# Four edits at the program's end and in GpSimd's row chains of a four-layer graph kernel

## The chip, the cores and the metric

The kernel runs on one core of one Trainium2 chip. The metric is device time in microseconds (us) of one execution; of several runs the median is taken. Engines are named as in the profile: PE (TensorE), PEld (its weight loads), DVE (VectorE), ACT (ScalarE), POOL (GpSimd), SP (SyncE, which issues most DMAs).

## The reference, cut to what matters

Inputs are `x` [4096, 64] and a 0/1 adjacency matrix `adj` [4096, 4096], both float32. Four layers follow each other, each of the form `x = layernorm(x + L(x, adj))`:

```python
# layer 0: mean over neighbours
h = (adj @ x + x) / deg;  out = relu(concat([x, h]) @ W + b);  out = out / max(|out|, 1e-12)
# layers 1 and 3: attention in hyperbolic space (c = 1/r**2 in layer 1, c = 1 in layer 3)
x_t   = logmap0(x)
att   = sigmoid((x_t @ wl)[:, None] + (x_t @ wr)[None, :] + b) * adj          # [N, N]
local = logmap(x[:, None, :], x[None, :, :])                                  # every pair i, j
out   = proj(expmap(x, einsum('ij,ijd->id', att, local)))
# layer 2: neighbours weighted by 0.5 ** (their rank counted from the row's end), at most 100
out = w @ (x @ weight) + bias
```

`logmap` and `expmap` are made of dot products, norms, an artanh and a tanh. Per row of `x`, layers 1 and 3 so need sums over the 4096 neighbours (the heavy part), and after it a chain of operations on one number a row: three inverse square roots (of the tangent vector's squared norm, of the result's squared norm for `proj`, and of the variance for the layernorm), a tanh and a reciprocal.

## The kernel before

**Tiling.** The 4096 rows are 32 blocks of 128. The output rows are cut into four groups `s` of 1024 columns of the transposed adjacency matrix; a layer goes through them in the order 3, 2, 1, 0 (`GROUPS`). Within a group it goes through 16 pairs `g` of two blocks, `k = 1` and then `k = 0`. One load on SP's queue (`load`, six buffers) brings one pair's tile of `adj`, 128 x 2 x 1024 float32, 1 MB.

**A pair in layers 1 and 3** (`attend`, from L1064). For each of the two blocks PE fills a PSUM tile `z` of 128 x 1024 by six matmuls of 512 columns (L1098, L1101, L1104; there are three such tiles of two banks each). ACT makes `sig` (L1113) and the square `sq` of z (L1116); DVE makes t = max(z, 0) * sig (L1119). Once a pair, DVE completes both blocks together, t = (sq + const) * t, over 2048 columns (L1121). PE then multiplies t with the neighbours' rows and adds into the PSUM tile `acc` (`add_up`, L1076, four matmuls a pair, two pairs behind the current one; what is left over follows after the last pair). ACT copies the group's sums to SBUF (L1127, `sums`).

**The rows of a group** (`move`, L1137 to L1270). PE turns the sums into rows and centres them (L1168, in two parts through the one bank `aux`), ACT copies each part out (L1179), and then come w = x*u (L1184), u squared (L1185, ACT), their sums over 64 columns (L1187, L1189, DVE) and some 80 operations on 128 x 8 numbers: one for each row of the group. They end in two large products (L1265, L1266) and their sum (L1269), which is the next layer's `x` of that group. For the last group, 0, these operations run on DVE; for groups 3, 2 and 1 the small ones and the large products run on GpSimd (class `Small`, whose `stt` is two GpSimd operations at L749 and L750), save the reductions, the reciprocal (L1233) and the seed of each root (L762), which stay on DVE. In a root, L766 to L774 are the Newton steps; `rsqrt` (from L720) is the same root for the other rows on DVE, such as those of `prepare` and `norm_rows`, which make a layer's operands ready.

```python
def pool_done(small, large=0):           # units to wait for GpSimd
    if place[0] == 2:                    # place[0] is the layer
        return 2 + int((small * 0.29 + large) / 1.45)
    return 2 + int(small * 0.33 + large)
...
def soon():
    return 0 if place[0] in (0, 2) else 1
```

**Order of the work.** PE's and ACT's instructions run in the order in which the program issues them; the order on DVE and GpSimd is a scheduler's, held behind the pairs. The pair loop calls `tick` after each block and each pair. Each call advances the row work, which is written as Python generators in two queues (`later`, `in_turn`): the number that a generator yields is the number of ticks until its next piece is issued. In layers 1 and 3 `near()` and `soon()` are one tick; `pool_done(small, large)`, and `Small.wait` through it, estimate from numbers of small and large GpSimd operations how many ticks to leave before DVE or ACT needs their result. `free` waits until the bank `aux` is not held. So a group's chain is issued among the pairs of the next group; that of group 0 of layer 3 has nothing beside it.

**Around it.** Layer 2 makes its supports (`supports`, L1298 to L1319) as groups of layer 1 become ready, and its own rows (`end_2`, L1556 among others, a 256-column product with a PSUM operand). After layer 3 each group's rows are stored (`store`, L1692 to L1695: groups 1 and 0 on SP's queue, 3 and 2 on ACT's). The program's end also has a check, `fits` (L1706 to L1719), transposed by PE (L1733) and loaded into a register that decides a branch.

Of the kernel before, what the change touches and what calls it, by code (L numbers as in the profile page):

```python
# [49 lines left out]

LN2 = 0.6931471805599453
ROOT2 = 2.0**0.5
LOG = (0.3333341, 0.1998662, 0.14984541)
OFF_EDGE = 255.0
CUT = 27.0
# [5 lines left out]
def gnn_stack_kernel(  # L61
# [509 lines left out]
    def stream(fits):  # L571

        with ExitStack() as st:
# [74 lines left out]
            def soon():  # L648


                return 0 if place[0] in (0, 2) else 1
# [7 lines left out]
            def near():  # L659

                return 3 if place[0] == 0 else 1
# [58 lines left out]
            def rsqrt(a, name):  # L720

                n = a.shape[1]
                r, t = nums(name, n), nums("rs_t", n)
                V.tensor_scalar(
                    r.bitcast(I32), a.bitcast(I32), -0.5, float(0x5F3759DF), ALU.mult, ALU.add
                )
                for _ in range(3):
                    V.tensor_mul(t, r, r)
                    V.scalar_tensor_tensor(t, t, -0.5, a, ALU.mult, ALU.mult)
                    V.scalar_tensor_tensor(r, t, 1.5, r, ALU.add, ALU.mult)  # L730
                return r

            class Small:
# [18 lines left out]

                def wait(self, small, large=0):

                    return pool_done(small, large) if self.on_pool else soon()

                def rsqrt(self, a, name, small):

                    r, t = self.nums(name), self.nums("rs_t")
                    if self.on_pool:  # L760
                        yield self.wait(small)
                    V.tensor_scalar(  # L762
                        r.bitcast(I32), a.bitcast(I32), -0.5, float(0x5F3759DF),
                        ALU.mult, ALU.add,
                    )
                    for _ in range(3):  # L766
                        self.mul(t, r, r)
                        if self.on_pool:
                            self.mul(t, t, a)
                            self.ts(t, t, -0.5, 1.5, ALU.mult, ALU.add)  # L770
                            self.mul(r, t, r)
                        else:
                            self.stt(t, t, -0.5, a, ALU.mult, ALU.mult)
                            self.stt(r, t, 1.5, r, ALU.add, ALU.mult)  # L774
                    return r


# [286 lines left out]
            def attend(layer, s, rate, then):  # L1064

                left_b = left_bs[s]

                acc = ps.tile([P, W], F32, name="acc")
                lag = []

                def add_up(g, t, behind=None):

                    for k in (1, 0):
                        j = 2 * g + k
                        for h in range(2):
                            it = nc.tensor.matmul(  # L1076
                                acc[h * D : (h + 1) * D, :], xe[:, j, :],
                                t[:, k, h * W : (h + 1) * W],
                                start=j == BLOCKS[0], stop=j == BLOCKS[-1],
                            )  # L1080
                            if behind is not None:
                                in_order(it.ins, behind.ins)

                for g in reversed(range(NB // 2)):
                    _, edge = load(s, g)
                    need((layer, 2 * g // WB))
                    if g == 4 and then is not None:
                        later(in_turn((layer, then, "left"), spread_left(then)), True)
                    for k in (1, 0):
                        j = 2 * g + k  # L1090
                        of = slice(j * P, (j + 1) * P)

# [14 lines left out]
                        if k == 1:  # L1107
                            if len(lag) == 2:
                                add_up(*lag.pop(0), last)
                            sq = sb.tile([P, 2, WW], F32, name="sq")  # L1110
                            t = sb.tile([P, 2, WW], F32, name="t", bufs=3)
                        sig = sb.tile([P, WW], F32, name="sig", bufs=3)
                        nc.scalar.activation(  # L1113
                            sig, left_b, AF.Sigmoid, bias=right[:, j : j + 1]
                        )
                        nc.scalar.activation(  # L1116
                            sq[:, k], zp, AF.Square, bias=ROOT + OFF, scale=-1.0 / UNIT
                        )
                        V.scalar_tensor_tensor(t[:, k], zp, 0.0, sig, ALU.max, ALU.mult)  # L1119
                        tick(rate)  # L1120
                    V.scalar_tensor_tensor(t, sq, HIGH**2, t, ALU.add, ALU.mult)  # L1121
# [5 lines left out]
                nc.scalar.copy(sums, acc)  # L1127
                return sums
# [8 lines left out]
            def move(layer, s, sums, curve):  # L1137
# [55 lines left out]
                G.mul(k, k, rb[:, at])  # L1193

# [68 lines left out]
                G.mul(q, q, r)  # L1263
                yield soon()
                E.tensor_mul(w, xg, over(p))  # L1265
# [519 lines left out]
```

## Time and profile before

| what | us |
|---|---|
| median of 3 runs (lowest to highest) | 1074.26 (1074.15 to 1074.6) |
| the profiled execution, its own time | 1069.06 |
| its span | 1067.3 |
| busy in the span: PE / PEld / DVE / ACT / POOL | 982.1 / 403.2 / 920.2 / 754.3 / 270.8 |
| mean granted PE clock | 0.971 |
| DMA traffic | 271.62 MB, 254 GB/s |

In the span, layer 0 takes about 0 to 198 us, layer 1 to 517, layer 2 to 717 and layer 3's pairs to 1038; the last row chain and the store follow. The span is the part of the execution that the profiler's records cover; 1.76 us of the execution's own time lie around it. The profiled execution is a single one, 5.2 us shorter than the median of the runs; lengths of instructions are read from it, and differences are formed against its own time.

A line of the timeline gives start, duration, engine, line, operation, output<-inputs with their shapes, and in brackets the engine's idle time before it with the releaser, the instruction that ended the wait. A line of the table by stretch gives the stretch and its length, the busy time and count of instructions of PE, PEld, DVE, ACT and POOL, the mean granted PE clock (1.00 is full speed), the mean share of the 16 DMA engines and GB/s. Line numbers are those of the kernel before, unless the text says otherwise.

### The profile page before, as it was taken

To read this page: it belongs to the slowest core of one execution; us is meant where nothing else is said; L and a number is where in the kernel's file an instruction comes from. 1 tells how busy PE (TensorE), PEld (TensorE's weight loads), DVE (VectorE), ACT (ScalarE), POOL (GpSimd) and SP (SyncE) were. 2 spreads that over 40 slices of the span, in tenths; PEclk is the share of its full clock that TensorE was granted. 3 is DMA by queue.
4 is the path that set the end of the run, shared out by engine and by line. 5 is a ranking of instruction groups with operands and counts; after the bars stand their busy time and mean duration, and the time that the engine had idled before them with its cause. 6 is when DMAs were issued, how large, how long until landed. Compare 5 with 4: busy or idle time off the path is not lost.

```text
span 1067.3 us, 13569 instructions
## 1 busy us (share of the span) xinstructions
PE 982.1 (92%) x4760; PEld 403.2 (38%) x4845; DVE 920.2 (86%) x1501; ACT 754.3 (71%) x877; POOL 270.8 (25%) x649
## 2 busy tenths in 40 slices
PE   5997998789999999999999999998899999999980
PEld 2454554333333333333333344443333333333320
DVE  8577887899999999999485489849999999999976
ACT  0013122779988899888677788898898888898850
POOL 0011212010044515435500010101102454444163
PEclk8899999989999999999999999999999999999985
DMA  9999999745656656757598999996465766666300
GB/s 364 356 426 364 383 395 375 277 175 197 233 204 230 215 206 202 249 184 249 205 363 332 371 346 316 324 321 222 138 236 190 250 216 208 241 228 234 131 1 24
DMA packets 38580, 271.62 MB, mean 254 GB/s; under 512 B 4710, under 2 KB 4710, under 8 KB 5734
## 3 DMA queue, kind: packets, MB, share of 16 engines
q1 hardware_dynamic: 37728, 270.03, 69.3%
q8 instruction: 40, 0.66, 0.2%
q10 hardware_dynamic: 774, 0.63, 0.2%
q14 instruction: 38, 0.31, 0.1%
HBM read 269.58 MB, written 1.05 MB: 254 GB/s over the span
## 4 chain that ended last, share of the span: by engine, by line
PE 66%; DVE 22%; ACT 5%; DMA 2%; POOL 2%; issue 2%; ACTq 0%; SPq 0%; POOLq 0%
PE acc L1076 17%; PE z L1641 11%; PE z L1101 8%; PE z L1098 7%; PE z L1104 7%; DVE t L1119 7%; DVE t L1121 6%; PE acc L1465 6%; PE z L1653 3%; DVE junk L844 2%; PE z L1607 2%; DMA edges<-in_adj_dram 2%; ACT sq L1648 1%; ACT sq L1116 1%; POOL sq L1435 1%
## 5 line engine op out<-in xcount | busy, mean ns | idle before, releaser
L1119 DVE SCALAR_TENSOR_TENSOR t<-z,sig 128x1024 f32<-128x1024 f32 x256 | 309.7, 1218 | 16.9 <-ACT sq L1116 14.9
L1121 DVE SCALAR_TENSOR_TENSOR t<-sq,t 128x2048 f32<-128x2048 f32 x128 | 295.2, 2306 | 0.2
L1116 ACT ACTIVATE sq<-z 128x1024 f32<-128x1024 f32 x256 | 254.3, 1021 | 56.5 <-PE z L1104 21.6
L1113 ACT ACTIVATE sig<-left_b,right 128x1024 f32<-128x1024 f32 x256 | 286.9, 1149 | 5.3 <-DVE t L1119 4.5
L1076 PE MATMUL acc<-t,xe 128*64 128x512 f32 x1024 | 260.4, 614 | 10.9 <-DVE t L1121 9.3
L1101 PE MATMUL z<-lo_hi,hi_lo 128*128 128x512 f16 x512 | 193.7, 378 | 3.8 <-issue 0.9
L1104 PE MATMUL z<-dst,src 74*128 74x512 f16 x512 | 194.7, 380 | 0.0
L1098 PE MATMUL z<-edges,two_i 128*128 128x512 bf16 x463 | 181.7, 392 | 5.4 <-DVE t L1119 5.4
L1648 ACT ACTIVATE sq<-z 128x512 bf16<-128x512 f32 (+1 forms) x192 | 137.6, 740 | 40.1 <-PE z L1641 39.5
L1076 PEld LDWEIGHTS acc<-t,xe 128*64 128x64 f32 x1024 | 64.3, 137 | 140.6 <-issue 106.5
L1098 PEld LDWEIGHTS <-two_i 128*128 128x128 bf16 x512 | 50.2, 98 | 120.7 <-issue 74.5
L1465 PE MATMUL acc<-edges,first 128*128 128x512 bf16 x241 | 77.9, 400 | 16.5 <-DMA edges<-in_adj_dram 15.9
L1641 PE MATMUL z<-edges,pass_by 128*128 128x512 bf16 x240 | 84.7, 388 | 7.3 <-ACT sq L1648 6.0
L844 DVE SCALAR_TENSOR_TENSOR t<-edges 128x2048 bf16<-128x2048 f32 x32 | 73.0, 2287 | 19.6 <-DMA edges<-in_adj_dram 19.2
L1641 PE MATMUL z<-edges,enter 128*128 128x512 bf16 x251 | 86.8, 387 | 0.5
L844 DVE SCALAR_TENSOR_TENSOR junk<-edges 128x2048 bf16<-128x2048 f32 x32 | 73.1, 2284 | 13.1 <-DMA edges<-in_adj_dram 13.1
L1465 PE MATMUL acc<-edges,third 128*65 128x512 bf16 x256 | 80.9, 397 | 0.8 <-issue 0.2
L1104 PEld LDWEIGHTS <-src 74*128 74x128 f16 x512 | 49.1, 96 | 72.0 <-issue 9.2
L1101 PEld LDWEIGHTS <-hi_lo 128*128 128x128 f16 x512 | 50.2, 98 | 60.6 <-issue 14.5
L901 POOL TENSOR_TENSOR sq<-z 128x512 f32<-128x512 f32 x8 | 10.2, 1278 | 156.1 <-DVE z L900 144.8
L1184 POOL TENSOR_TENSOR w_att<-x,u 128x512 f32<-128x512 f32 x6 | 12.7, 2121 | 140.9 <-ACT u L1179 140.9
L1607 PE MATMUL z<-sq,halves 128*128 128x512 bf16 x120 | 45.1, 377 | 0.7 <-ACT sq L1648 0.5
(399 smaller groups left out, 965.0 us busy)
## 6 DMA issues: line engine op xcount, KB each, us to landing
edges<-in_adj_dram SPq DMA_DIRECT2D x256, 1024.0 KB, 4.9
x<-in_x_dram SPq DMA_DIRECT2D x4, 256.0 KB
out_dram<-x ACTq DMA_DIRECT2D x2, 256.0 KB
out_dram<-x SPq DMA_DIRECT2D x2, 256.0 KB
w_sb<-in_L_gnn_W_dram ACTq DMA_DIRECT2D x1, 32.0 KB, 4.8
w_twice<-in_L_gnn_weight_dram ACTq DMA_DIRECT2D x2, 16.0 KB, 4.8
given<-in_L_gnn_b_dram ACTq DMA_DIRECT2D x1, 0.2 KB
given<-in_L_gnn_bias_dram ACTq DMA_DIRECT2D x1, 0.2 KB
```

The lines of the kernel that those rows point to most:

```text
L844: V.scalar_tensor_tensor(junk, a, 0.0, a, ALU.not_equal, ALU.not_equal, accum_out=odd[:, n : n + 1])
L1076: it = nc.tensor.matmul(acc[h * D : (h + 1) * D, :], xe[:, j, :], t[:, k, h * W : (h + 1) * W], start=j == BLOCKS[0], stop=j == BLOCKS[-1],)
L1098: nc.tensor.matmul(half, two_i, edge[:, at : at + W], start=True, stop=False)
L1101: nc.tensor.matmul(half, hi_lo[:, of], lo_hi[:, to], start=False, stop=False)
L1104: last = nc.tensor.matmul(half, src[:, of], dst[:, to], start=False, stop=True)
L1113: nc.scalar.activation(sig, left_b, AF.Sigmoid, bias=right[:, j : j + 1])
L1116: nc.scalar.activation(sq[:, k], zp, AF.Square, bias=ROOT + OFF, scale=-1.0 / UNIT)
L1119: V.scalar_tensor_tensor(t[:, k], zp, 0.0, sig, ALU.max, ALU.mult)
L1121: V.scalar_tensor_tensor(t, sq, HIGH**2, t, ALU.add, ALU.mult)
L1465: nc.tensor.matmul(accs[h][:m], lhs[:, j, :], edge[:, at : at + W], start=j == BLOCKS[0], stop=j == BLOCKS[-1],)
L1641: nc.tensor.matmul(z[:, h : h + W], lhs, rhs[:, h : h + W], start=j == BLOCKS[0], stop=True, skip_group_check=True,)
L1648: weighed[0] = nc.scalar.activation(w, z[:, :n], AF.Exp, bias=-(OFF_EDGE + CUT) * LN2, scale=-LN2)
```

## The change

Four edits, in the diff's order of lines:

- *Roots.* Each inverse square root starts from the same integer seed, and takes one step of third order and one Newton step where it took three Newton steps: seven DVE operations after the seed for nine, ten GpSimd operations for twelve.
- *Counts.* In layers 1 and 3 `Small.wait` gives fewer ticks for the same GpSimd work, and two `soon()` after the second reduction are left out for chains on GpSimd.
- *The last pair.* In the last pair of the last group of layer 3, block 0 gets a tile `t` of its own; L1121's operation becomes two of 1024 columns, and each half is added up on its own.
- *The last sums.* For group 0 of layer 3 (`straight`) the row sums go into two `z` tiles, one for each part, in place of two turns of `aux`. The square and the product w = x*u read PSUM in two parts each; only the column of the total is copied out (`sum_1`); the last product with q reads PSUM again.

The diff, cut to its core:

```diff
+THIRD = 0.375**0.5
 # rsqrt(a, name), on DVE
-                for _ in range(3):
-                    V.tensor_mul(t, r, r)
-                    V.scalar_tensor_tensor(t, t, -0.5, a, ALU.mult, ALU.mult)
-                    V.scalar_tensor_tensor(r, t, 1.5, r, ALU.add, ALU.mult)
+                V.tensor_mul(t, r, r)
+                V.scalar_tensor_tensor(t, t, THIRD, a, ALU.mult, ALU.mult)
+                V.scalar_tensor_tensor(t, t, -10.0 / 3.0 * THIRD, t, ALU.add, ALU.mult)
+                V.scalar_tensor_tensor(r, t, 5.0 * THIRD**2, r, ALU.add, ALU.mult)
+                V.tensor_mul(t, r, r)
+                V.scalar_tensor_tensor(t, t, -0.5, a, ALU.mult, ALU.mult)
+                V.scalar_tensor_tensor(r, t, 1.5, r, ALU.add, ALU.mult)
 # Small.wait
-                    return pool_done(small, large) if self.on_pool else soon()
+                    if not self.on_pool:
+                        return soon()
+                    if place[0] == 2:
+                        return pool_done(small, large)
+                    return 1 + int((small * 0.29 + large * 1.04 + 2.3) / 1.6)
 # Small.rsqrt (on DVE: as in rsqrt above)
-                    for _ in range(3):
+                    self.mul(t, r, r)
+                    if self.on_pool:
+                        s = self.nums("rs_s")
+                        self.mul(t, t, a)
+                        self.ts(s, t, 0.375, -1.25, ALU.mult, ALU.add)
+                        self.mul(t, t, s)
+                        self.ts(t, t, 1.875, None, ALU.add)
+                        self.mul(r, t, r)
                         self.mul(t, r, r)
-                        if self.on_pool:
-                            self.mul(t, t, a)
-                            self.ts(t, t, -0.5, 1.5, ALU.mult, ALU.add)
-                            self.mul(r, t, r)
...
+                        self.mul(t, t, a)
+                        self.ts(t, t, -0.5, 1.5, ALU.mult, ALU.add)
+                        self.mul(r, t, r)
 # attend
-                def add_up(g, t, behind=None):
-                    for k in (1, 0):
+                def add_up(g, t, ks, behind=None):
+                    for k in ks:
...
+                            ts = [t, t]
+                            if g == 0 and then is None and layer == 3:
+                                ts[0] = sb.tile([P, 2, WW], F32, name="t", bufs=3)
...
-                        V.scalar_tensor_tensor(t[:, k], zp, 0.0, sig, ALU.max, ALU.mult)
+                        V.scalar_tensor_tensor(ts[k][:, k], zp, 0.0, sig, ALU.max, ALU.mult)
                         tick(rate)
-                    V.scalar_tensor_tensor(t, sq, HIGH**2, t, ALU.add, ALU.mult)
-                    lag.append((g, t))
+                    if ts[0] is t:
+                        V.scalar_tensor_tensor(t, sq, HIGH**2, t, ALU.add, ALU.mult)
+                        lag.append((g, t, (1, 0)))
+                    else:
+                        for k in (1, 0):
+                            V.scalar_tensor_tensor(
+                                ts[k][:, k], sq[:, k], HIGH**2, ts[k][:, k], ALU.add, ALU.mult
+                            )
+                            lag.append((g, ts[k], (k,)))
 # move
-                for part in range(2):
+                straight = last and layer == 3
+                parts = []
+                if straight:
...
+                    for part in range(2):
+                        t = z_tile()[:, : 4 * (D + 1)].rearrange(
+                            "p (i h f) -> p i h f", i=2, h=2
+                        )
+                        for i in range(2):
+                            cols = slice((2 * part + i) * P, (2 * part + i + 1) * P)
+                            nc.tensor.matmul(
+                                t[:, i], sums[:, cols], centre, start=True, stop=True
+                            )
+                        parts.append(t)
+                    yield near()
+                    for part, t in enumerate(parts):
+                        nc.scalar.activation(part_of(sq, part), t[:, :, :, :D], AF.Square)
+                        V.tensor_mul(part_of(w, part), part_of(xg, part), t[:, :, :, :D])
+                    for part, t in enumerate(parts):
+                        nc.scalar.copy(
+                            sum_1.rearrange("p (h k) -> p k h", h=2)[
+                                :, 2 * part : 2 * part + 2
+                            ],
+                            t[:, :, :, D],
+                        )
+                    yield near()
+                for part in () if straight else range(2):
...
-                E.tensor_mul(w, xg, u)
-                nc.scalar.activation(sq, u, AF.Square)
-                yield G.wait(0, 1) if G.on_pool else near()
+                if not straight:
+                    E.tensor_mul(w, xg, u)
+                    nc.scalar.activation(sq, u, AF.Square)
+                    yield G.wait(0, 1) if G.on_pool else near()
...
                 V.tensor_reduce(d, w, AX.X, ALU.add)
-                yield soon()
-                yield soon()
+                if not G.on_pool:
+                    yield soon()
+                    yield soon()
...
                 E.tensor_mul(w, xg, over(p))
-                E.tensor_mul(u, u, over(q))
+                if straight:
+                    for part, t in enumerate(parts):
+                        V.tensor_mul(part_of(u, part), t[:, :, :, :D], part_of(over(q), part))
+                else:
+                    E.tensor_mul(u, u, over(q))
```

More of the change, by code (lines that the diff above doesn't have):

```diff
@@ L765, in rsqrt @@
                     )
-                    for _ in range(3):
-                        self.mul(t, r, r)
-                        if self.on_pool:
-                            self.mul(t, t, a)
-                            self.ts(t, t, -0.5, 1.5, ALU.mult, ALU.add)
-                            self.mul(r, t, r)
-                        else:
-                            self.stt(t, t, -0.5, a, ALU.mult, ALU.mult)
-                            self.stt(r, t, 1.5, r, ALU.add, ALU.mult)
+                    self.mul(t, r, r)
[6 more added lines that the diff above has]
+                        self.mul(r, t, r)
+                        self.mul(t, r, r)
+                        self.mul(t, t, a)
+                        self.ts(t, t, -0.5, 1.5, ALU.mult, ALU.add)
+                        self.mul(r, t, r)
+                    else:
+                        self.stt(t, t, THIRD, a, ALU.mult, ALU.mult)
+                        self.stt(t, t, -10.0 / 3.0 * THIRD, t, ALU.add, ALU.mult)
+                        self.stt(r, t, 5.0 * THIRD**2, r, ALU.add, ALU.mult)
+                        self.mul(t, r, r)
+                        self.stt(t, t, -0.5, a, ALU.mult, ALU.mult)
+                        self.stt(r, t, 1.5, r, ALU.add, ALU.mult)
                     return r
@@ L1162, in move, with part_of @@
                     u, sum_1 = all_u[:, :, :D], all_u[:, :, D]
-                for part in range(2):
+                straight = last and layer == 3
+                parts = []
+                if straight:
+                    def part_of(rows, part):
+                        of = slice(2 * part, 2 * part + 2)
+                        return rows.rearrange("p (h k) f -> p k h f", h=2)[:, of]
+                    for part in range(2):
[21 more added lines that the diff above has]
+                for part in () if straight else range(2):
                     yield from free()
@@ L1265, in move @@
                 E.tensor_mul(w, xg, over(p))
-                E.tensor_mul(u, u, over(q))
+                if straight:
+                    for part, t in enumerate(parts):
+                        V.tensor_mul(part_of(u, part), t[:, :, :, :D], part_of(over(q), part))
+                else:
+                    E.tensor_mul(u, u, over(q))
                 yield soon()
```

## The prediction

> **What bounds the kernel now.** I read the table of engine times by stretch first, then the timeline of the last 47 us, then the chain of waits. In the columns of the table: the stretch, its length, then busy time and instruction count of PE, PEld, DVE, ACT and POOL, the granted PE clock, the DMA share, GB/s.
>
> ```profile
> 860.00:950.00 90.00, 88.77 (x389) 31.73 (x395) 88.03 (x63) 80.13 (x84) 39.43 (x94) 1.00 0.64 222
> ...
> 1034.50:1038.30 3.80, 3.68 (x8) 0.77 (x8) 0.35 (x4) 0.00 (x0) 3.03 (x17) 0.50 0.00 0
> 1038.30:1044.80 6.50, 2.84 (x9) 1.94 (x9) 2.16 (x6) 1.97 (x4) 4.87 (x23) 0.50 0.00 1
> 1044.80:1060.00 15.20, 0.00 (x0) 0.00 (x0) 13.45 (x77) 0.21 (x1) 4.84 (x12) 0.50 0.07 22
> 1060.00:1062.10 2.10, 0.00 (x0) 0.00 (x0) 2.03 (x5) 0.00 (x0) 0.00 (x0) 0.50 0.00 0
> 1062.10:1067.30 5.20, 0.00 (x0) 0.00 (x0) 0.00 (x0) 0.00 (x0) 0.00 (x0) 0.50 0.15 57
> ```
>
> In the pairs of layers 1 and 3 (first line) PE and DVE are both about 98% busy: work only reordered there is worth little. From 1034.5 on nothing overlaps: one chain of small steps, and every step removed from it moves the end. These lines of the timeline carry it (start, duration, engine, line; in brackets idle time before it and who ended it):
>
> ```profile
> 1024.24 2.28 DVE L1121 SCALAR_TENSOR_TENSOR t<-sq,t 128x2048 f32<-128x2048 f32 x1
> 1024.35 2.22 POOL L1227 TENSOR_TENSOR y<-xy,y 128x8 f32<-128x8 f32 x1
> ...
> 1034.61 3.68 PE L1076 MATMUL acc<-t,xe 128*64 128x512 f32 x8 [1.01 <-DVE g L1718]
> ...
> 1038.34 0.58 ACT L1127 COPY sums<-acc 128x512 f32<-128x512 f32 x1 [9.79 <-PE acc L1076]
> ...
> 1042.00 0.38 ACT L1179 COPY ys<-aux 128x260 f32<-128x260 f32 x1 [1.38 <-PE aux L1168]
> ...
> 1042.64 0.17 DVE L762 TENSOR_SCALAR n<-w 128x8 int32<-128x8 int32 x1 [5.49 <-POOL w L1260]
> ...
> 1044.82 0.23 DVE L747 SCALAR_TENSOR_TENSOR k<-d,k_c,ys 128x8 f32<-128x8 f32 x1
> ...
> 1046.97 1.06 POOL L1265 TENSOR_TENSOR w_att<-x,p 128x512 f32<-128x512 f32 x1
> ...
> 1047.16 0.90 DVE L767 TENSOR_TENSOR rs_t<-r_t 128x8 f32<-128x8 f32 x1
> ...
> 1062.09 0.35 SPq L1695 DMA_DIRECT2D out_dram<-x  x1
> ```
>
> To see: the last group's row chain (group 0, on DVE) runs from 1044.82 to 1062.06, then the store and the end. Before it two chains arrive almost together: PE and ACT (last sums, copies, done at 1042.38), and GpSimd's unfinished chain of group 1, for whose L1260 DVE sits blocked until 1042.64. GpSimd's three large operations then (1046.97 to 1050.3) stretch three small DVE operations from 0.17 to 0.90, 0.96 and 1.03 us.
>
> [...] POOL L1227 takes 2.22 us beside L1121 where its neighbours take 0.20, and the three DVE operations above are stretched. [...] in the waits, DVE L1119 waits 14.9 us in all for ACT L1116, which reads the same z. [...] Here eight L1076 records take 1.94 us in the loop and 3.68 at the end (clock 0.50).
>
> **The change, part by part.** Times are from the timeline of before; the instruction order is that of the changed program as built.
>
> 1. *Last pair by unit.* L1121 of the last pair (1032.32 to 1034.55) becomes two half operations, block k=1 first. L1119 (1.22 us for 1024 columns) is the nearest row: about 1.15 each, so 1032.2 to 1033.4 and to 1034.5. PE ends the pair before at 1033.6, then does k=1's half at half clock (1.84) to 1035.4 and k=0's to 1037.3, against 1038.29 now. **-1.0.** At full clock the saving is the same. The extra t tile needs the buffer that the add-up at 1026.72 to 1028.66 reads, free well ahead of its write at 1031.
>
> 2. *Sums from two PSUM tiles.* Now, from the end of the sums copy (S = 1038.92): matmuls, ACT copy, matmuls, ACT copy, square 0.63, two reductions; k starts at S+5.90. Changed: four matmuls in a row, 2 x 1.24 at half clock, to S+2.53 (a second z tile takes away the wait for the first copy); the second square of 256 columns (0.38, as L1179) to S+2.97; then, [...] DVE's second product (0.41, as L1556, 256 columns with a PSUM input) to S+3.43, its successor starting at S+3.40; reductions 0.59 and 0.70 apart; k at S+4.69. **-1.2.** ACT's two copies of sum_1 wait for that product but are 0.5 us ahead of k. L1733 now stands before these matmuls on PE, beside ACT's 0.58 us copy: nothing. L1266 becomes two PSUM products[...]; the trace has 0.41 for L1556, steps of 0.35 and 0.4 against 0.64 now: **+0.1.**
>
> 3. *Third-order roots.* On DVE a root has 7 operations after its seed, not 9. The last chain has three roots at 0.20 us a step (1054.73 to 1056.33 is eight steps): 3 x 2 x 0.20 = **-1.2.** The other 22 roots on DVE lose two operations each, 0.08 a step between pair operations: those in layer 0 lie beside loads and PE; some four at each start of layers 1 and 3, where the chain runs through DVE (720 to 758), give **-0.4**, taken with part 5.
>
> 4. *Shorter counts, two yields fewer, GpSimd roots of 10 operations instead of 12.* By order of issue on DVE the last seed of group 1 in layer 3 moves from behind all 384 pair operations to behind number 376, 12.7 us of pair operations (1.2 and 2.2 each) ahead of their end, so about 1021.8. Ten root operations of 0.28, two more, then 1.04+1.04+1.19, with one or two catches of 2 us behind L1121: done at 1030 to 1032.5. So DVE is no longer blocked to 1042.64 (this is what lets part 2 show) and the three stretched operations fall to 0.2 a step: 0.73+0.80+0.87 = **-2.4.** What is late next is PE's half-clock chain. The store of group 1 goes out ahead of the value load on SP some 15 us sooner; SP has no load left to delay. Group 2's store on ACT's queue moves up too; its x is due eight pair operations before it. The casts and matmuls of L1303 to L1319 move with their groups.
>
> 5. *The same chains inside the loop.* The tail of group 1 (three large GpSimd operations) in layers 1 and 3 now falls among pair operations. Before, two of four such tails stretched one L1121 (3.15 against 2.28). Price: 0 to 0.9 each, half of it likely, and PE's queue of z absorbs some: **+0.4**, cancelling the -0.4 of part 3.
> The shortened waits: from the d reduction to the first seed DVE now has 5.8 us of pair work, GpSimd needs 2.9; from reciprocal to seed n 5.8 to 9.2 against 4.5 with one catch; from n to w 9.2 to 12.6 against 6.9 with one catch and 8.9 with two. All hold; a second catch in the first two costs 0 to 2 us, behind which the next pair's L1119 and so PE's z would queue. I take 0.
>
> Sum: -1.0 - 1.2 + 0.1 - 1.2 - 2.4 = **-5.7**, rounded to -5.6 for a store and program end (5.2 us) left as they are. Against the profiled execution's own time, 1069.06 (span 1067.3 and 1.76 around it), 1063.5. The runs' median is 5.2 us higher, 1074.26, and nothing in the cut parts explains that gap, so I carry the difference over: **1068.7.**
>
> **The rivals.** (a) *As summed*, 1068.7, by itself 1067.3 to 1070.3: 0.60.
> (b) *The clock comes back.* [...] if PE has full clock for the last half add-up and the four sum matmuls, 0.9 and 1.2 us more are gone: 1066.6. [...] 0.13.
> (c) *The edits cover each other.* One link, such as the order of readers in part 2 or a stretched L1121 just before the end, takes back about 2 us: 1070.8. 0.10.
> (d) [...] All six GpSimd tails stretch an L1121, four more than now, 3.6 us: 1072.2, on the edge of no change. For it: GpSimd is caught one to three times in each stretch. Against: PE waited for L1121 only 0.6 us from 780 to 1030 with two such tails. 0.10.
> (e) *Slower: counts too short.* [...] if a seed or reciprocal (L762, L1233) comes before GpSimd is ready, pairs stop behind it. There are 24 such waits in six chains, 2 us for each extra catch. One miss in each chain is 12 us: 1080.6. It takes over from no change at four misses on the path. For it: DVE waited 2.3 and 5.5 us in such places at both layer ends. Against: those stood outside the loop with no spacing, and the spacings above have room. 0.07.
> That the roots or the split don't take effect can be excluded: the instructions stand in the built program.
>
> **How the numbers follow.** Some 0.2% (2.1 us) is what a measurement of this kernel can tell from no change. (a), (b), (c) and half of (d) are faster beyond it: 0.88. The other half of (d) and a sliver of (e) are no change: 0.06. The rest of (e) is slower: 0.06. The range goes from 1066.0, under (b), to 1071.8, between (c) and (d).
>
> **What would show it.** In the profile of the changed kernel: from the last L1121 half to the last add-up's end some 2.8 us instead of 3.7; k less than 5 us after the sums copy; no DVE operation of 128x8 over 0.3 us in the last chain, which then takes about 11.6 us from k to the large products instead of 15.2; GpSimd idle after its last large operation near 1032. It is wrong if DVE shows waits for POOL at L762 or L1233 inside the loop, if GpSimd still runs when k starts, or if the pair loop of layers 1 or 3 is longer by more than 2 us.

## The result, and the profile after

The changed kernel takes **1067.93 us** (median of 8 runs, 1065.31 to 1071.28), the kernel before 1073.71 (8 runs, 1070.35 to 1074.6): ratio 0.9961, 95% interval 0.9941 to 0.9981, so 2.0 to 6.3 us less; the two medians differ by 5.8. The forecast was 1068.7. The profiled execution took 1067.64 (span 1065.9).

The table of engine times by stretch, for the stretches that answer to those of before: 90 us of pairs in layer 3, last add-ups, sums to k, the chain, the large products, store and end.

```profile
866.00:956.00 90.00, 89.71 (x392) 31.55 (x392) 87.15 (x64) 78.57 (x83) 46.20 (x105) 1.00 0.64 221
1039.30:1042.80 3.50, 3.12 (x15) 0.54 (x11) 2.76 (x6) 0.00 (x0) 0.02 (x1) 1.00 0.19 75
1042.80:1046.80 4.00, 1.37 (x11) 0.99 (x9) 2.45 (x6) 1.68 (x5) 0.00 (x0) 1.00 0.03 6
1046.80:1058.40 11.60, 0.00 (x0) 0.00 (x0) 10.02 (x71) 0.21 (x1) 0.00 (x0) 0.57 0.01 4
1058.40:1060.60 2.20, 0.00 (x0) 0.00 (x0) 2.13 (x5) 0.00 (x0) 0.00 (x0) 0.50 0.00 0
1060.60:1065.90 5.30, 0.00 (x0) 0.00 (x0) 0.01 (x1) 0.00 (x0) 0.00 (x0) 0.50 0.16 56
```

The timeline of its end (L1143 and L1147 are the former L1121, L1094 the add-up, L1155 the sums copy, L1333 GpSimd's last large operation, L774 a root's first step):

```profile
1035.64 2.64 DVE L1143 SCALAR_TENSOR_TENSOR t<-sq,t 128x2048 f32<-128x2048 f32 x1
1036.21 3.11 POOL L1333 TENSOR_TENSOR x<-u,w_att 128x512 f32<-128x512 f32 x1
...
1039.33 2.34 DVE L1147 SCALAR_TENSOR_TENSOR t<-sq,t 128x1024 f32<-128x1024 f32 x2
...
1040.60 2.21 PE L1094 MATMUL acc<-t,xe 128*64 128x512 f32 x8 [0.33 <-DVE t L1147]
...
1042.86 0.59 ACT L1155 COPY sums<-acc 128x512 f32<-128x512 f32 x1 [7.43 <-PE acc L1094]
...
1046.84 0.23 DVE L751 SCALAR_TENSOR_TENSOR k<-d,k_c,ys 128x8 f32<-128x8 f32 x1
...
1048.52 0.17 DVE L774 TENSOR_TENSOR rs_t<-r_t 128x8 f32<-128x8 f32 x1
...
1058.40 0.69 DVE L1325 TENSOR_TENSOR y<-x,p 128x512 f32<-128x512 f32 x1
...
1060.64 0.35 SPq L1759 DMA_DIRECT2D out_dram<-x  x1
```

To see: GpSimd ends just as the last pair's operation begins; no small DVE operation is stretched (none of 128x8 over 0.23 us from 1046.84 on); PE ran at full clock up to the last sums (1.00 in the stretches with matmuls). From the start of the last pair operation to the span's end it is 26.57 us, where before it was 34.98 (1032.32 to 1067.3): **8.4 us less, more than the 5.7 forecast**. Yet the last pair operation starts 7.0 us *later* (1039.33 for 1032.32), and so the two profiled spans differ by 1.4 us only. So the forecast time alone proves little; the question is what took those 7 us.

To answer it I took from each profile the starts of the first 127 pair operations (of 128; with the last pair split, 127 are whole), and from them the length of each stretch. The kernels are those of the experiments below.

| start of pair operation, us | 1st | 1st to 16th | 16th to 64th (layer 1) | 64th to 65th (layer 2) | 65th to 81st | 81st to 127th (layer 3) | 127th to end |
|---|---|---|---|---|---|---|---|
| before | 197.85 | 83.96 | 231.05 | 209.50 | 86.75 | 219.70 | 38.49 |
| before, again | 201.44 | 85.01 | 231.06 | 209.51 | 86.81 | 219.70 | 38.57 |
| before, filled gap | 198.51 | 83.52 | 231.05 | 209.75 | 87.86 | 219.69 | 38.52 |
| end alone | 201.87 | 85.28 | 231.09 | 209.55 | 86.74 | 219.72 | 37.85 |
| roots alone | 197.15 | 82.77 | 230.70 | 209.24 | 87.28 | 219.74 | 36.72 |
| roots, rows alone | 196.51 | 83.66 | 231.10 | 209.23 | 87.07 | 219.97 | 38.46 |
| roots, chains alone | 201.10 | 82.97 | 230.65 | 209.51 | 87.82 | 219.47 | 36.88 |
| counts alone | 198.21 | 84.29 | 230.92 | 216.97 | 86.46 | 221.17 | 33.88 |
| changed | 198.00 | 83.61 | 231.30 | 212.87 | 88.48 | 221.38 | 30.26 |
| changed, no end | 197.62 | 83.63 | 231.28 | 212.72 | 87.02 | 221.37 | 32.16 |
| changed, cast on DVE | 197.09 | 82.29 | 233.55 | 209.24 | 87.44 | 221.41 | 30.18 |
| counts in layer 3 only | 200.59 | 82.73 | 230.70 | 209.23 | 87.23 | 221.36 | 30.16 |
| counts, last chain only | 199.59 | 83.55 | 230.69 | 209.24 | 87.43 | 218.57 | 35.53 |
| the same, early start | 201.36 | 82.27 | 230.71 | 209.23 | 87.17 | 222.62 | 31.04 |

The first four rows are one program up to its last pairs. They agree within 0.1 us in layers 1 and 3 and within 0.25 in layer 2, and differ by 4.0 us where layer 0 ends, by 1.8 in the first 16 pairs and by 1.1 from the 65th to the 81st. The end agrees within 0.1 us in the first three; the fourth has the split end. So the columns for layers 1, 2, 3 and the end can be compared from single profiles; the other three cannot. In the four that can, the change brings **+0.25, +3.37, +1.68 and -8.23**, together -2.9; the other three differ by +1.5 in these two profiles.

### The profile page after: what moved, and what is told of

It reads as the page before. It is cut to its first block, busy times and chain, and to the rows that moved or that the text cites. A ratio compares the mean times of both kernels' runs of the same rounds, so it can differ in the third digit from the quotient of the medians.

```text
span 1065.9 us, 13575 instructions
## 1 busy us (share of the span) xinstructions
PE 987.6 (93%) x4845; PEld 401.2 (38%) x4845; DVE 912.4 (86%) x1448; ACT 755.0 (71%) x878; POOL 288.9 (27%) x613
## 4 chain that ended last, share of the span: by engine, by line
PE 68%; DVE 20%; ACT 5%; DMA 3%; issue 1%; POOL 1%; ACTq 0%; SPq 0%; POOLq 0%; DVEq 0%
PE acc L1094 17%; PE z L1705 11%; PE z L1116 8%; PE acc L1529 7%; PE z L1122 7%; DVE t L1140 7%; PE z L1119 7%; DVE t L1143 7%; PE z L1717 3%; DMA edges<-in_adj_dram 3%; PE z L1671 2%; ACT sq L1137 2%; ACT sq L1712 1%; DVE junk L862 1%; PE aux L996 1%
## 5 line engine op out<-in xcount | busy, mean ns | idle before, releaser
L1143 DVE SCALAR_TENSOR_TENSOR t<-sq,t 128x2048 f32<-128x2048 f32 x127 | 294.3, 2317 | 0.2
L1094 PE MATMUL acc<-t,xe 128*64 128x512 f32 x1024 | 261.4, 612 | 10.1 <-DVE t L1143 9.6
L1116 PE MATMUL z<-edges,two_i 128*128 128x512 bf16 x512 | 201.3, 393 | 7.5 <-DVE t L1140 7.5
L1094 PEld LDWEIGHTS acc<-t,xe 128*64 128x64 f32 x1024 | 64.5, 137 | 140.1 <-issue 107.7
L862 DVE SCALAR_TENSOR_TENSOR t<-edges 128x2048 bf16<-128x2048 f32 x32 | 73.4, 2304 | 28.6 <-DMA edges<-in_adj_dram 28.2
L1529 PE MATMUL acc<-edges,first 128*128 128x512 bf16 x256 | 80.2, 395 | 18.2 <-DMA edges<-in_adj_dram 18.1
L1705 PE MATMUL z<-edges,pass_by 128*128 128x512 bf16 x248 | 87.0, 390 | 6.3 <-ACT sq L1712 5.7
L862 DVE SCALAR_TENSOR_TENSOR junk<-edges 128x2048 bf16<-128x2048 f32 x32 | 73.1, 2284 | 15.2 <-DMA edges<-in_adj_dram 15.2
L1243 POOL TENSOR_TENSOR w_att<-x,u 128x512 f32<-128x512 f32 x6 | 18.1, 3013 | 179.9 <-ACT u L1237 179.9
L1671 PE MATMUL z<-sq,halves 128*128 128x512 bf16 x128 | 48.1, 377 | 0.5 <-ACT sq L1712 0.5
```

The source lines that it names most:

```text
L862: V.scalar_tensor_tensor(junk, a, 0.0, a, ALU.not_equal, ALU.not_equal, accum_out=odd[:, n : n + 1])
L1094: it = nc.tensor.matmul(acc[h * D : (h + 1) * D, :], xe[:, j, :], t[:, k, h * W : (h + 1) * W], start=j == BLOCKS[0], stop=j == BLOCKS[-1],)
L1116: nc.tensor.matmul(half, two_i, edge[:, at : at + W], start=True, stop=False)
L1529: nc.tensor.matmul(accs[h][:m], lhs[:, j, :], edge[:, at : at + W], start=j == BLOCKS[0], stop=j == BLOCKS[-1],)
L1705: nc.tensor.matmul(z[:, h : h + W], lhs, rhs[:, h : h + W], start=j == BLOCKS[0], stop=True, skip_group_check=True,)
```

## The experiments

A ratio is against runs of the kernel before on the same chip (medians 1070.49 to 1071.31 in the three sets); the runs of one kernel lie 4 to 14 us apart, so ratios resolve some 2 us with 13 or more runs, 3 with six; a single run settles no total, and from it only the stretches of its profile are used. Where an edit is a part of the diff shown above, it is named and not repeated.

**Roots alone** (the diff of the two `rsqrt` and `THIRD`, nothing else).

> The kernel before with the third-order roots alone. Both theories: the last row chain loses six DVE operations of 0.20 us, so k to the large products takes 14.0 us where it took 15.2 (the stretch of three DVE operations beside GpSimd's large ones stays, since GpSimd's chain of group 1 gets only 1.7 us shorter); the first pair operation of layer 3 stays at 722 to 723 us. About -1.2 us in all, ratio 0.9989.

Measured: 1066.41, ratio 0.9961 (0.9946 to 0.9976). k to the large products takes 13.97 us (15.22): -1.25, as expected. k comes 0.5 us sooner after the last pair operation's start (12.02 for 12.50), since GpSimd's chain is shorter, and in layer 1 0.35 us go. The profile's columns give -2.3, the runs -2.6 to -5.8; three later experiments look at the rest.

**Counts alone** (the diff of `Small.wait`, and the two yields).

> The kernel before with the shorter counts alone. Theory A (the 3.4 us that layer 2 of the changed kernel is longer come from the counts: the cast of x_hl on GpSimd is moved beside a DVE pass of 2.29 us, and PE's queue stands behind it): the first L1121 of layer 3 starts some 3.4 us later than before's 722.36, the end gains 2.4 to 3 us, and the sum is +0 to +3 us, ratio 1.000 to 1.003. Theory N (the longer layer 2 is the chance of one profiled execution in a stage that the loads bound): layer 3 starts at 722 to 723 us, the sum is -2.4 us, ratio 0.9978.

Measured: 1069.52, ratio 0.9984 (0.9965 to 1.0003). In its profile layer 2 is 7.5 us longer, the end 4.6 shorter (of this 2.45 from k to the large products, 12.77 for 15.22). So the profile shows theory A's loss, at twice its size, and layer 3 began at 730.39 us, not at theory N's 722 to 723. GpSimd's cast in its timeline, on both occasions that fall into layer 2:

```profile
544.19 3.18 POOL L1309 TENSOR_TENSOR x_hl<-x,x_hl 128x512 f16<-128x512 f32 x1 [29.77 <-ACT x_hl L1308]
572.02 3.27 POOL L1309 TENSOR_TENSOR x_hl<-x,x_hl 128x512 f16<-128x512 f32 x1 [24.66 <-ACT x_hl L1308]
```

Beside each runs a DVE pass over the loads (L848, 2.29 us), begun 0.13 and 0.03 us before the cast; in the kernel before all four casts took 1.16 us. Call a cast of over 3 us beside such a pass a collision. Two collisions here cost 7.5 us; the changed kernel has one, and lost 3.4. The runs don't bear the total out: the four columns of this profile add up to +4.2, but the runs lie between 3.7 us less and 0.3 more, nearer to theory N's ratio than to theory A's. Perhaps not every execution collides twice; this wasn't shown, as only one has a profile. The profiled execution took 1073.61, 4.1 us above the median.

**End alone** (the diff in `attend` and the `straight` part).

> The kernel before with the last pair by unit and the sums from two PSUM tiles, roots and counts as before. All up to the last pair is unchanged, so its pair operations show how far one profile differs from another: theory A expects less than 1 us at the last pair, theory N several us at layer 2's end. At the end -1.0 for the last pair; of the 1.2 for the sums some, as DVE stands before the seed of group 1's last root until GpSimd is done, and the three stretched operations stay: -1.0 to -2.2 us, ratio 0.998 to 0.999. If the last matmuls run at full clock in this kernel too, the order of the end makes it, and the end gains up to 2 us more; if at half clock, the clock comes from somewhere else.

Measured: 1070.46, ratio 1.0 (0.9983 to 1.0016). The pairs repeat those of before within 0.1 us. At the end:

```profile
1036.59 5.38 PE L1076 MATMUL acc<-t,xe 128*64 128x512 f32 x16 [2.50 <-DVE t L1125]
...
1048.46 0.17 DVE L762 TENSOR_SCALAR n<-w 128x8 int32<-128x8 int32 x1 [3.18 <-POOL w L1301]
...
1049.33 0.23 DVE L747 SCALAR_TENSOR_TENSOR k<-d,k_c,ys 128x8 f32<-128x8 f32 x1
```

DVE still stands 3.18 us, until GpSimd's L1301 (the former L1260) is done, so the end gains only 0.6 us: less than the -1.0 to -2.2 expected. The 16 matmuls took 5.38 us, where the changed kernel has 1.94 and 2.21 for them. I read this as half clock in part, so the question of the clock stayed open here.

**Counts in layer 3 only** (changed kernel):

```diff
-                    if place[0] == 2:
+                    if place[0] != 3:
                         return pool_done(small, large)
...
-                if not G.on_pool:
+                if not G.on_pool or layer == 1:
                     yield soon()
```

> The changed kernel with the old counts in layers 1 and 2, the shorter ones in layer 3 alone. Theory A: layer 2 gets its 3.4 us back (the first pair operation of layer 3 starts at about 722 to 723 us where it was 725.78), the end keeps its gain, so about 1064.5 us, ratio to before 0.991. Theory N: 1068, ratio 0.996, as the changed kernel.

Measured: **1062.12**, 6 runs, ratio 0.992 (0.989 to 0.995). Layer 2 takes 209.23 us, the end keeps its gain: theory A for layer 2. The loss in layer 3 stays. The profile's columns differ from the changed kernel's by -0.60, -3.64, -0.02 and -0.10.

**Roots of the rows alone** (of the diff, `THIRD` and the part in `rsqrt`, on DVE).

> The kernel before with the third-order roots in rsqrt alone (the rows' norms, prepare and the layernorms), the roots of the hyperbolic chains left as they were. Theory A (roots alone gained 4.2 us though the end's profile shows 1.8, because the root steps of layer 0's row chains and of the first groups of layers 1 and 3 are on the path): -2 to -3 us, ratio 0.997 to 0.998, and the 16 pairs of the first group of layer 1 (first to last pair operation) take some 82.7 us, as with all roots new, where the kernel before took 84.0. Theory N (the 4.2 us are the chance of the runs; only the last chain counts): no change, ratio 1.000.

Measured: 1070.21, ratio 1.0003 (0.9983 to 1.0023). Theory A's -2 to -3 us lie outside the interval (-1.8 to +2.5 us), so it falls: these roots gain nothing measurable. The first 16 pairs (83.66 us) decide nothing: one program alone varied from 83.52 to 85.28 there.

**Cast on DVE** (changed kernel):

```diff
-                nc.gpsimd.tensor_sub(hl[:, :, D:], xg, hl[:, :, :D])
+                V.tensor_sub(hl[:, :, D:], xg, hl[:, :, :D])
```

> The changed kernel with the difference for x_hl in the supports on DVE, where GpSimd did it. Theory A (layer 2 is longer since GpSimd's cast stands 3.3 us beside a DVE pass, and PE's queue behind it): the first pair operation of layer 3 comes 2.5 to 3.4 us sooner after the last one of layer 1 than in the changed kernel, whose distance is 212.9 us (before 209.5). Theory B (the place of the supports in PE's queue costs it, whichever engine casts): the distance stays near 213.

Measured: 1063.02 in one run; layer 2 takes 209.24 us. Theory A, in one profile: the supports stand at the same place among PE's matmuls, and only the engine of the cast differs (0.69 us on DVE). In layer 1 this kernel is 2.25 us longer than the changed one; two casts of 0.68 us on DVE fall there, and the rest was not explained. The timeline of the changed kernel at the collision, whose L1368 is the cast, L862 a DVE pass over the loads and L1373 the transposes behind it:

```profile
542.98 2.29 DVE L862 SCALAR_TENSOR_TENSOR t<-edges 128x2048 bf16<-128x2048 f32 x1 [0.77 <-DMA edges<-in_adj_dram]
543.00 3.28 POOL L1368 TENSOR_TENSOR x_hl<-x,x_hl 128x512 f16<-128x512 f32 x1 [30.22 <-ACT x_hl L1367]
...
546.34 0.86 PE L1373 MATMUL aux<-ident,x_hl 128*128 128x128 f16 x8 [2.15 <-DVE un L751]
```

DVE began 0.02 us before GpSimd and took its usual 2.29 us; the cast took 3.28. PE stood 2.15 us (the wait is put down to DVE; what came last was the cast's end at 546.28), and the loads, whose buffers PE frees, fell behind. By stretch in the changed kernel, then in the kernel before:

```profile
540.00:550.00 10.00, 7.85 (x42) 3.02 (x40) 8.67 (x29) 5.01 (x8) 3.28 (x1) 0.83 0.86 310
550.00:560.00 10.00, 10.00 (x71) 3.87 (x68) 5.42 (x35) 7.27 (x8) 0.00 (x0) 1.00 0.67 258
```

```profile
540.00:550.00 10.00, 9.94 (x57) 3.67 (x55) 9.00 (x39) 6.24 (x8) 0.00 (x0) 1.00 0.98 388
550.00:560.00 10.00, 9.94 (x61) 3.91 (x62) 9.08 (x37) 7.16 (x8) 1.16 (x1) 1.00 0.96 357
```

The last two columns show it: DMA share 0.67 against 0.96, 258 GB/s against 357 in the second stretch. Over the 60 us from 520 to 580 it is 317 GB/s against 339 (341 with the cast on DVE; layer 2 starts at 512.9 in all three), so 1.3 MB were not loaded by then. At the layer's mean of 333 GB/s (517 to 717 us of before) they stand for some 4 us by estimate, near the 3.4 us lost. PE's clock fell as well, to a mean of 0.83 in the first stretch; how much of the loss is due to that was not separated.

That the loss follows the collisions shows in the table's other rows too. The eleven profiles in which no cast on GpSimd took more than 1.39 us have 209.23 to 209.75 us in layer 2, the two with one collision 212.72 and 212.87, the one with two 216.97. Of the two with one collision, the next kernel is the changed program up to its last pair, yet there the other cast was caught:

```profile
542.62 1.16 POOL L1368 TENSOR_TENSOR x_hl<-x,x_hl 128x512 f16<-128x512 f32 x1 [30.22 <-ACT x_hl L1367]
567.08 3.17 POOL L1368 TENSOR_TENSOR x_hl<-x,x_hl 128x512 f16<-128x512 f32 x1 [23.30 <-ACT x_hl L1367]
```

So which cast meets a pass varies from execution to execution.

**Changed, no end:**

```diff
-                            if g == 0 and then is None and layer == 3:
+                            if False:
...
-                straight = last and layer == 3
+                straight = False
```

> The changed kernel without its two edits at the end: last pair whole, sums through aux and ACT copies; roots and counts as changed. Theory A (the two edits gain 2.1 us once GpSimd is out of the way; in the kernel with the end alone they were hidden behind it): from the start of the last L1121 to the span's end some 28.4 to 28.7 us, where the changed kernel has 26.6. Rival (the counts and the clock alone made the end short): within 0.5 us of 26.6.

Measured: 1067.49 in one run; 28.36 us from the last pair operation's start to the end (26.57 in the changed kernel).

```profile
1039.79 1.94 PE L1094 MATMUL acc<-t,xe 128*64 128x512 f32 x8 [1.52 <-DVE g L1782]
1041.77 0.58 ACT L1155 COPY sums<-acc 128x512 f32<-128x512 f32 x1 [8.34 <-PE acc L1094]
...
1046.91 0.23 DVE L751 SCALAR_TENSOR_TENSOR k<-d,k_c,ys 128x8 f32<-128x8 f32 x1
```

The last pair operation began at 1037.44. To the add-up's end: 4.29 us against 3.48 with the split (-0.8). From the copy's end (1042.35) to k: 4.56 against 3.39 (-1.17). Large products to store: 2.06 against 2.24 (+0.18). Theory A in kind, a little below its 2.1: the end edits are worth 1.8 us once GpSimd is out of the way.

**Counts for the last chain only** (changed kernel; `self.short` is the last argument of `Small`):

```diff
-                    if place[0] == 2:
+                    if not self.short:
                         return pool_done(small, large)
...
-                G = Small(not last, "_1" if last else "")
+                G = Small(not last, "_1" if last else "", layer == 3 and s == 1)
...
-                if not G.on_pool:
+                if not G.short:
                     yield soon()
```

> The changed kernel with the shorter counts, and without the two yields, for one chain only: group 1 of layer 3, the last on GpSimd. Theory A (the counts gain at the end, and cost 3.4 us in layer 2 and 1.4 in layer 3's other chains, whose large GpSimd operations stretch a pair operation): 1.4 us less than with the counts in all of layer 3, about 1060.7 us, ratio 0.990 to 0.991; no pair operation near the 110th is stretched to over 3 us. Rival (the chains' place in layer 3 costs nothing): 1062, ratio 0.992.

Measured: 1066.33, ratio 0.9948 (0.9925 to 0.997). From the 81st pair operation to the start of the last pair's it took 223.05 us, 2.0 less than with the counts in all of layer 3 (225.06), and no operation of 3 us is left. (In the table the difference is 2.8, as the 127th operation itself stands earlier in DVE's order here.) This part of theory A held. But GpSimd's large operations began only at 1044.50, and from the last pair's start the end took 31.05 us for 26.5, so the total fits neither expectation. Group 1's first seed on DVE comes behind 122 whole pairs, where it was 117: the chains stand in one queue, which the next experiment puts to the test.

**Early start** (the kernel just shown, and):

```diff
-                yield pool_done(15, 3) if G.on_pool else after(72)
+                yield (1 if layer == 3 else pool_done(15, 3)) if G.on_pool else after(72)
```

> As the kernel with the shorter counts for one chain only, and in layer 3 the last wait of a GpSimd chain, 11 us of pairs, is cut to one unit. Theory A (the chain of group 1 came too late there since the chains stand in one queue, and each starts when the last wait of the one before is over): GpSimd's large operations end before the last pair operation, from the last L1121 to the end 26.5 us, the loop of layer 3 (first to 127th pair operation) 306 to 308.6 us, about 1060 to 1062 us, ratio 0.990 to 0.992. Rival (group 1's chain is late for another reason): the end stays at 31 us, 1066.

Measured: 1065.41, 6 runs, ratio 0.9929 (0.9903 to 0.9956). The first seed is back behind 117 pairs and the last large operation ends at 1037.05; theory A for the cause. But the 81st to 127th pair took 222.62 us (all of layer 3's loop 309.8, over the 306 to 308.6 expected; what cost it was not taken apart), and the end 27.35 for the 26.5 expected; PE did its 16 last add-up matmuls in 5.35 us, where the changed kernel has 1.94 and 2.21. It isn't shown to be better than the counts in layer 3 only.

**Roots of the chains alone** (of the diff, `THIRD` and the part in `Small.rsqrt`).

> The kernel before with the third-order roots in the hyperbolic chains alone, rsqrt as before. Theory A (only the last chain counts; the 4.2 us measured with all roots are partly the chance of the runs): -1.3 to -2 us, ratio 0.998 to 0.999, the end 33.2 us after the last L1121 starts, as with all roots. Rival (the roots in these chains are worth 4 us, in a place that the profiles don't show): ratio 0.996.

Measured: 1068.97, ratio 0.997 (0.9955 to 0.9985); the end 33.38 us, k to the large products 14.08. The columns give -2.2, the interval -1.6 to -4.8. The end has theory A's size (33.2 expected). The runs' interval holds the upper part of theory A and the rival's 4 us, so they don't decide between the two. With the rows' roots at nothing measurable, the gain of the roots lies in the chains as far as these runs can tell.

**The kernel before, again** (no edit).

> The kernel before, once more, as any other run. Both theories: ratio 1.000; how far its ratio lies from 1 says what the other ratios are worth. Its profile shows which stretches repeat: theory A expects the pairs of layers 1 and 3 and the end to repeat within 0.5 us, and layer 0 to differ by some us.

Measured: ratio 1.0007 (0.999 to 1.0023). Its end:

```profile
1035.86 1.94 PE L1076 MATMUL acc<-t,xe 128*64 128x512 f32 x8 [2.49 <-DVE t L1121]
...
1039.32 1.94 PE L1076 MATMUL acc<-t,xe 128*64 128x512 f32 x8 [1.52 <-DVE g L1718]
...
1047.35 0.17 DVE L762 TENSOR_SCALAR n<-w 128x8 int32<-128x8 int32 x1 [5.49 <-POOL w L1260]
...
1049.53 0.23 DVE L747 SCALAR_TENSOR_TENSOR k<-d,k_c,ys 128x8 f32<-128x8 f32 x1
```

The same program had full clock this time: 1.94 and 1.94 us, where the first profile has 3.68 for the last eight matmuls and, for the eight before,

```profile
1031.15 2.44 PE L1076 MATMUL acc<-t,xe 128*64 128x512 f32 x8 [2.49 <-DVE t L1121]
```

Yet k stands 12.50 us behind the last pair operation's start in both (1037.03 to 1049.53; 1032.32 to 1044.82). So PE's half clock did not set the end, GpSimd's chain did: DVE waited 5.49 us for it at either clock.

**Filled gap** (before, and):

```diff
+                if layer == 3 and then is None:
+                    zp = z_tile()
+                    for n in range(8):
+                        nc.tensor.matmul(
+                            zp[:, n % 2 * W : (n % 2 + 1) * W], hi_lo[:, :P], lo_hi[:, :W],
+                            start=True, stop=True,
+                        )
                 for args in lag:
                     add_up(*args)
```

> The kernel before with eight more matmuls of 512 columns into a spare z tile after the last pair's z, ahead of the last two add-ups, where PE stood idle 2.5 us; nothing reads them. Theory C[...]: the last add-ups take 1.94 us each and end some 1.7 us sooner, the L1168 groups 0.6 us; the end is 1 to 2.5 us shorter, as far as DVE isn't held by GpSimd's chain to its 10.3 us after the last L1121's start. Rival[...]: half clock there as before, 1.9 us longer at most.

Measured: 1070.6 in one run. The add-ups took 1.94 us each, k came 12.50 us after the last pair operation's start again. As the kernel before also had 1.94 us for each when run again, this doesn't show whether the added matmuls had a part in it; what brings the half clock was not shown.

## Why the prediction was right, and where it wasn't

The total was right: 1068.7 forecast, 1067.93 measured. In part this was luck: two errors of its working offset each other.

- *Last pair, -1.0*, and *sums, -1.2 and +0.1*: -0.8, -1.17 and +0.18 measured (changed with and without the end). That DVE's products come behind ACT's squares held in the trace (DVE stood 1.16 us until ACT's L1211), and the two last products that read PSUM took 0.88 us together, where the one of before (L1266) took 0.68; the steps of 0.35 and 0.4 were an estimate. Right, though measured at full clock where the sum took half, and right that step 4 must first clear the way: alone they were worth 0.6.
- *Roots, -1.2 in the last chain*: -1.25 and -1.14. The -0.4 at the layer starts can't be told from chance: the columns there vary by 1 us and more. Not in the sum: GpSimd's chain ends 0.5 us sooner, which shows only while it decides, and 0.35 to 0.40 us go in layer 1 (roots alone, chains alone).
- *Stretched operations, -2.4*: -2.45 (counts alone). "11.6 us from k to the large products" was 11.56.
- **First error, in step 4.** The sum took GpSimd's chain and PE's to arrive "almost together" (1042.64 and 1042.38) and gave the wait almost nothing. The second number was at half clock. At full clock, with GpSimd out of the way, k comes 9.47 us after the last pair operation's start (changed, no end: 1037.44 to 1046.91), against 12.50: **3.0 us**, where the sum had 0.26. That is the 2.1 us of rival (b), whose 0.13 was an estimate, and more; but the change didn't bring the clock back: in 13 of the 14 profiles the sum matmuls ran at full clock (0.71 us for four or 1.16 for eight, where the first profile has 1.24 for four), those of the kernel before, run again, among them. In four of the 13 PE was busy with the last 16 add-up matmuls for 5.35 to 5.40 us, where it was 3.88 in the kernel before, run again, and 4.15 with the split in the changed one; the sums behind them were at full clock. The forecast was worked out from the one profile with the sums at half clock.
- **Second error, in steps 4 and 5.** "The casts and matmuls of L1303 to L1319 move with their groups" was priced at nothing, without naming what hides them. One cast on GpSimd met a DVE pass, and layer 2 lost **3.4 us**. The profile of before had shown the like in the pair loop (L1227, 2.22 us beside L1121, where its neighbours took 0.20), and the prediction did not carry it over to this place: here DVE began first and took 2.29 us, and the cast took 3.28 for 1.16. In layer 3 the columns show **+1.7**, and in layer 1 +0.25 (+0.6 against the old counts with the same roots), where +0.4 was written for both. Stretched pair operations explain only some 0.5 of the 1.7: between the 81st and 127th the changed kernel has one of 2.71 and one of 3.27 us (begun just after GpSimd's L1333), the kernel before one of 3.15. The rest I did not take apart.
- Rival (e) did not come: DVE shows no wait for L770 (the former L762) or L1293 inside the loops. Rival (d) came at half of its size: all six GpSimd tails stretched a pair operation, by 0.36 to 0.99 us each, 3.6 in all, where two were stretched before, by 1.8 in all. A sign of being wrong that the prediction named came as well: layer 3's loop, from the 65th to the 127th pair operation, is 3.4 us longer than before (309.86 for 306.45), with more than 2 named. In the changed kernel without its end, the same program up to there, it is 1.9 longer.

Added up: -8.2 at the end for -5.7, +5.3 in the layers for 0. The measured 2.0 to 6.3 us hold both the -2.9 of these columns and the forecast.

Counts in layer 3 alone keep the end and leave layer 2 as it was: 1062.12 us, ratio 0.992, the lowest median, with an interval that overlaps the changed kernel's a little, and those of the two kernels with the counts for one chain widely. The roots alone reached the ratio of the whole change, 0.9961: within what the runs can tell, the other three edits together added nothing measurable, as in the profile the layers took back much of what the end gained.

## What to carry to other kernels

When work is moved to make room at the end, price every place where it lands: a 1.16 us cast, for which one weight load had waited 0.5 us, cost 3.4 us in a layer whose loads kept the DMA engines 92% busy (517 to 717 us of before). Where two chains seem to arrive together, ask at which clock each was measured; the one that varies least from run to run may be the one that decides. Cut a profile at a repeated operation and compare the stretches: those that repeat within 0.1 us can settle from one profile what runs 5 us and more apart cannot. But run the unchanged program more than once to know which stretches repeat, and remember that a profile is one execution: with the counts alone it showed a loss that the runs don't bear out.

## What was not expected of the hardware

The same program had its last two add-ups at 2.44 and 3.68 us in one execution and at 1.94 and 1.94 in another, with the same idle time of PE before the first of them (2.49 us in both). One program's first pair operation behind layer 0 began at 197.85 to 201.87 us, while its pairs in layers 1 and 3, behind the first 16 of each, repeated within 0.1 us. The cast on GpSimd took 1.16 us in the kernel before and, begun 0.02 to 0.14 us behind a DVE pass of 2.29, 3.17 to 3.28 in three others.
